# A conv, attention and expert kernel: the last half image's norm and gates moved into the experts, gate rows as single passes, constants made in layer 1

## The chip, the cores and the metric

The kernel runs on one core of a Trainium2 chip. Its time is the device time of one execution in microseconds. Three runs of the kernel before gave 3234.16, 3236.74 and 3243.24 us, median 3236.74. The profile shows one further execution, and every time of a single instruction here comes from that one.

## The reference, cut to what matters

Layer 0 is a convolution and attention block on 8 images of 256 channels and 32 x 32 points. Layer 1 works on 1024 tokens of 256 features per image: a causal attention, and then a mixture of 8 experts in which every token goes through every expert:

```python
t = t + attn(ln(t), WQ, WK, WV)
z = ln(t)
w = softmax(mean(z, axis=0) @ Wr + br)        # mean over the 8 images: one gate per token place and expert
h = relu(bn1(z @ W1[e] + b1[e]))
h = relu(bn2(h @ W2[e] + b2[e]))
t = t + sum_e w[:, e] * (h @ Wo[e] + bo[e])
```

The gate w needs the second norm z of all 8 images, because it is made from their mean. So the last image's second norm and the gate stand between the attention and the first gated product.

## The kernel before, in words

Tokens lie along the free axis, features on 128 partitions in KC = 2 groups; HALF = 512 tokens are half an image. Most operations go through a recording helper, so the profile shows them all at line 72, and they are told apart by their tiles.

**Layer 1** (from line 1276) takes the images in turn. `together` (446) runs two generators: `causal(b)` or `last()`, which is scores, softmax, transposes and product of image b, and beside it `beside(b)` (1558): the next image's first norm and keys, the previous image's second norm, and `chores`. A step's yielded number is its estimated cost, and the ratio 0.85 sets how much of the second generator goes between steps of the first. The order of the instructions on PE, DVE, ACT and POOL is the order of these calls. `layer_norm` (1342) transposes tokens onto partitions (`tpt`), takes mean and variance on DVE (`st`, `mv`), computes one over the root on POOL (`y`, `r`), scales (`zt`), and transposes back (`tpz`). `second_norm` (1418) adds the result to `feat` on POOL and gives it to `z_parts` (1432), which splits each number into an upper part (ACT), a lower part and a difference (DVE), so that a product of full precision is made of single-pass products; the three parts go to DRAM (`z_d`). `expert_parts` (1313) does the same for the experts' weights, by way of `we` and `parts_w`, as the 20 `chores`.

For the last image there is no next one to work beside. Its second norm is cut in two by `second_norm_half` (1442): half 0 and `gate(0)` (1532) are run beside the last attention products, and half 1 and `gate(1)` after everything else (1592 to 1594). `gate(h)` makes the scores `lg` (three products of 8 columns for each 128 tokens, in full fp32), a softmax over 8 experts on DVE and ACT, transposes it (`pwT`), and copies it into `wT`, 8 rows by 1024 tokens, in fp32.

**The experts** (from line 1609) first make `sel8` on POOL and `boT` by two transposes `pbo`. `sel8` holds, for each expert, an 8 x 128 matrix with ones in the expert's row: `gate_rows` (1663) multiplies it with `wT`, so that an expert's gates come to stand on all 128 partitions (`pw`, copied to `wb`). `gated_bias` (1670) multiplies `boT` with `wT` (`pg`, copied to `gb`). The folded norm constants `s1`, `s1a` and so on are written in this part of the program, but the scheduler had moved them to the start of layer 1.

Work is then 128 pieces: 2 groups of 4 experts, 2 halves, 8 images (32 visits of a half image), 4 experts in each. Piece n runs `layer1` of itself, `layer2` of piece n - 2 and `layer3` of piece n - 4, four steps each, interleaved; the DVE and ACT work that a step leaves goes into `soon`, for the same steps of the next piece. Each visit needs its z parts (`fetch_z`, tile `ze`, 1536 KB) and its t (`fetch_t`, tile `te`); visit 0's parts are loaded ahead into `z_first`. When a new half or group begins (b == 0), `gate_rows` is called at the start of its four pieces. PSUM has two banks of `pm` for layer 2, `pw` and `pg` together, and one each of the two `pa` (layer 1).

Tile pools stand in the way of early loads: the pools of the experts take the memory of layer 1's pools, so the first load into them waits until layer 1's last reader is done. The weights for (expert 0, all layers) and (expert 1, layer 1) and `z_first` lie in a pool of their own (`wm`) and are loaded before.

## Time and profile before

| | |
|---|---|
| median of three runs | 3236.74 us |
| the profiled execution | 3235.5 us |
| its span, first to last instruction | 3233.8 us |
| mean granted PE clock | 0.964 |
| PE busy | 2962.3 us (92%), 16822 instructions |
| DVE busy | 2385.1 us (74%), 3002 instructions |
| ACT busy | 1569.5 us (49%), 2312 instructions |
| POOL busy | 337.9 us (10%), 410 instructions |
| DMA | 237.46 MB, mean 73 GB/s |

Layer 1 runs from about 1428 to 2071 us, the experts from 2096.55 us to the end. Where a stretch of the profile is given as `A:B`, A and B are us from the span's start; after them come its length, then for PE, weight loads on PE, DVE, ACT and POOL the busy us with the number of instructions, then the mean granted clock, the share of the DMA engines and GB/s. A row of the timeline gives start, duration, engine, operation, output tile, inputs, shape and count, and in brackets the idle time ahead of it and what ended it.

### The profile page before, as it was taken

The page shows a single profiled execution, that of the slowest core. Times are in us where ns is not written, and L with a number is a line of the kernel's source. Part 1 is how long each engine was busy: PE and PEld are TensorE (multiplying, and loading weights), DVE is VectorE, ACT ScalarE, POOL GpSimd, SP SyncE. Part 2 cuts the span into 40 slices and gives each one's busy share as a digit, 9 for nine tenths or more (in the row PEclk, how much of TensorE's full clock was granted, in tenths as well). Part 3 has the DMA queues.
Part 4 walks back from the last instruction along what each step waited for, and adds up shares of the span by engine and source line. Part 5 has one row for each costly group of instructions (what it writes and reads, how often), then busy time and mean ns, then how long its engine had stood idle before and what let it go on. Part 6 is the DMA issues. An engine that isn't in the chain of part 4 may idle for free.

```text
span 3233.8 us, 41619 instructions
## 1 busy us (share of the span) xinstructions
PE 2962.3 (92%) x16822; PEld 1941.5 (60%) x16822; DVE 2385.1 (74%) x3002; ACT 1569.5 (49%) x2312; POOL 337.9 (10%) x410
## 2 busy tenths in 40 slices
PE   5998899989898999859999999799999999999998
PEld 3654545454555555435666555577767777777776
DVE  1378778777877878655666655488878888887887
ACT  1554455545445445313333333266656666666665
POOL 1121111121212110001122222100000000000000
PEclk9999999999999999989999999799999999999999
DMA  4203030303030300011323311322211242221220
GB/s 149 62 19 79 27 79 27 79 27 79 27 79 27 79 14 8 17 71 69 142 112 118 124 79 52 136 111 86 78 66 66 92 139 103 91 72 65 84 80 26
DMA packets 60061, 237.46 MB, mean 73 GB/s; under 512 B 5382, under 2 KB 13654, under 8 KB 50774
## 3 DMA queue, kind: packets, MB, share of 16 engines
q1 hardware_dynamic: 59862, 234.74, 21.5%
q8 instruction: 134, 2.20, 0.3%
q14 instruction: 65, 0.53, 0.0%
HBM read 143.23 MB, written 91.49 MB: 73 GB/s over the span
## 4 chain that ended last, share of the span: by engine, by line
PE 45%; DVE 7%; ACT 2%; issue 1%; POOL 1%; DMA 0%; SPq 0%; POOLq 0%; ACTq 0%; DVEq 0%
PE pm L72 12%; PE pa L72 11%; PE q L72 11%; PE s L72 4%; PE po L72 3%; PE pv L72 2%; DVE nm L72 1%; DVE pr L72 1%; PE pk L72 1%; DVE parts L72 1%; DVE zt L72 1%; ACT pr L72 1%; DVE st L72 1%; PE tpt L72 1%; PE pw L72 1%
## 5 line engine op out<-in xcount | busy, mean ns | idle before, releaser
L72 PE MATMUL q<-h2p,w 128*128 128x512 f32 x1536 | 485.9, 425 | 2.9 <-DVE h2p L72 1.7
L72 PE MATMUL pa<-ze,w 128*128 128x512 f32 x1488 | 422.5, 392 | 0.0
L72 PEld LDWEIGHTS q<-h2p,w 128*128 128x128 f32 x1536 | 288.9, 188 | 118.2 <-issue 60.4
L72 DVE SCALAR_TENSOR_TENSOR x<-hpad,vec,x 128x1024 f32<-128x1024 f32 x248 | 317.1, 1283 | 39.9 <-ACT x L72 32.8
L72 DVE SCALAR_TENSOR_TENSOR conv<-hpad,vec,conv 128x1024 f32<-128x1024 f32 x256 | 329.3, 1293 | 13.8 <-ACT conv L72 7.2
L72 PEld LDWEIGHTS pa<-ze,w 128*128 128x128 f32 x1488 | 278.9, 188 | 69.8 <-issue 9.5
L72 ACT ACTIVATE h<-pa,bn_o,s1a 128x512 f32<-128x512 f32 x256 | 198.8, 777 | 203.4 <-PE pa L72 203.3
L72 ACT ACTIVATE pT<-s 128x1024 f32<-128x1024 f32 x256 | 247.4, 1024 | 69.1 <-PE s L72 69.1
L72 DVE SCALAR_TENSOR_TENSOR h<-pa,s1b,h 128x512 f32<-128x512 f32 x256 | 191.6, 749 | 113.2 <-PE pa L72 100.8
L72 PE MATMUL po<-pT,vT 128*32 128x256 f32 x4096 | 272.1, 383 | 0.0
L72 PE MATMUL ph<-xn,piw 128*128 128x512 f32 x512 | 244.4, 615 | 3.1 <-DVE xn L72 1.6
L72 PE MATMUL s<-kk,z 128*128 128x512 f32 x512 | 245.2, 609 | 0.9 <-DVE pr L72 0.9
L72 PE MATMUL pm<-h,w 128*128 128x512 f32 x512 | 242.0, 595 | 0.0
L72 PE MATMUL pm<-h1p,w 128*128 128x512 f32 x768 | 216.1, 389 | 0.5 <-DVE h1p L72 0.5
L72 DVE SCALAR_TENSOR_TENSOR o<-vpad,pe_w,o 128x1024 f32<-128x1024 f32 x128 | 163.5, 1282 | 45.2 <-ACT o L72 42.0
L72 PE MATMUL s<-qst,kst 128*128 128x256 f32 x1024 | 175.2, 313 | 14.2 <-DMA kst<-part 12.9
L72 ACT ACTIVATE hpad<-ph,pi_o 128x512 f32<-128x512 f32 x126 | 86.9, 690 | 182.4 <-PE ph L72 182.4
L72 ACT ACTIVATE h2p<-h 128x1024 fp32r<-128x1024 f32 x128 | 134.9, 1054 | 77.8 <-DVE h L72 77.8
L72 PEld LDWEIGHTS po<-pT,vT 128*32 128x32 f32 x4096 | 120.2, 110 | 84.5 <-issue 1.9
L72 PEld LDWEIGHTS s<-qst,kst 128*128 128x128 f32 x1024 | 136.8, 192 | 47.5 <-issue 42.4
L72 PEld LDWEIGHTS pm<-h1p,w 128*128 128x128 f32 x768 | 144.1, 188 | 31.5 <-DVE h1p L72 0.9
L72 PE MATMUL pz<-pow__116,hid 128*128 128x256 f32 x512 | 138.2, 426 | 27.1 <-DVE hid L72 27.1
(241 smaller groups left out, 4811.7 us busy)
## 6 DMA issues: line engine op xcount, KB each, us to landing
ze<-zd SPq DMA_DIRECT2D x31, 1536.0 KB, 6.3
zd<-parts SPq DMA_DIRECT2D x16, 1536.0 KB, 5.5
qst<-part SPq DMA_DIRECT2D x32, 512.0 KB, 8.5
kst<-part SPq DMA_DIRECT2D x32, 512.0 KB, 15.2
te<-ud SPq DMA_DIRECT2D x32, 512.0 KB, 3.9
wd<-parts_w SPq DMA_DIRECT2D x20, 768.0 KB, 3.6
w<-wd SPq DMA_DIRECT2D x20, 768.0 KB, 5.9
t<-in_x_dram SPq DMA_DIRECT2D x8, 1024.0 KB, 4.9
```

What stands on the lines that cost most here:

```text
L72: return self._tc.keep_in_program_order(method(*args, **kwargs))
```

## The change

- **Half 1 of the last image**: `last_norm` does only half 0, in layer 1, into `z2_last`; its z parts are no longer made there. Half 1's t is stored, and loaded again into `scratch` in the experts' phase. There `last_half` runs the same `layer_norm` and `gate(1)` as a generator, two steps in every even piece from piece 4 on, at the second and fourth of its four steps. Seventeen steps bring it to piece 20. `feat` becomes two tiles.
- **z parts of the last image** are made when its visits come (visit 7 for half 0, visit 15 for half 1): `fetch_z` leaves its three steps in `soon`, and stores them for the second expert group.
- **Gate rows**: `wT` has 32 rows, four copies (upper, lower, upper, lower part of the gates), in a format that PE multiplies in a single pass. `sel8` selects an upper and a lower row, and `boT` has upper, upper, lower, lower parts. `stacked` makes these. `gate_rows` and `gated_bias` are called after the piece's four steps and not ahead of them.
- **Constants**: `sel8`, `boT` and the folded constants are made in layer 1, partly in the chores. `mhalf1` moves to the lasting pool.
- **Memory**: `we` has one buffer instead of two. `z_parts` has two parts in its tile and writes the difference over its source; the store becomes two stores. The second buffer for layer 2's parts is `z_first`.

Cut: `layer_norm` and `gate` move out of layer 1's block with their source, rows and banks as arguments; their steps are unchanged but for `stacked` in `gate`.

```diff
-    wT = wm.tile([NE, N], F32, name="wT")
+    wT = wm.tile([4 * NE, N], F32R, name="wT")
+    feats = [None, wm.tile([P, KC, HALF], F32, name="feat1")]
+    z2_last = wm.tile([P, KC, HALF], F32, name="z2_last")
...
+    def stacked(dst, src, order):
+
+        first = [order.index(i) for i in range(2)]
+        dve.tensor_copy(dst[:, :, first[0]].bitcast(F32R), src)
+        dve.tensor_sub(dst[:, :, first[1]].bitcast(F32R), src, dst[:, :, first[0]])
+        for i, part in enumerate(order):
+            if i not in first:
+                dve.tensor_copy(dst[:, :, i], dst[:, :, first[part]])
...
+        ge4 = room([P, nt, 4, NE], "ge4", 1)
+        stacked(ge4, ge, (0, 1, 0, 1))
+        yield 1.0
+        pwT = bank([4 * NE, HALF], "pwT")
+        for i in range(nt):
+            pe.transpose(pwT[:, i * P : (i + 1) * P], ge4[:, i].rearrange("p a e -> p (a e)"), ident)
...
+        boT = wm.tile([4 * NE, KC, P], F32R, name="boT")
+        sel8 = wm.tile([4 * NE, NE, P], F32R, name="sel8")
+        sel = two.tile([4 * NE, NE, P], F32, tag="pT", name="sel")
+        nc.gpsimd.memset(sel, 0.0)
+        for part in range(2):
+            nc.gpsimd.affine_select(
+                out=sel, in_=sel, compare_op=ALU.not_equal, fill=1.0, base=-NE * part,
+                pattern=[[-1, NE], [0, P]], channel_multiplier=1,
+            )
+        nc.gpsimd.tensor_copy(sel8, sel)
...
-                    w_ = two.tile([P, KC, C], F32, tag="we", name="we")
+                    w_ = two.tile([P, KC, C], F32, tag="we", name="we", bufs=1)
...
+            stacked(bo4, cols("bo").rearrange("p (e g) -> p g e", g=KC), (0, 0, 1, 1))
+            pb = bank([4 * NE, KC, P], "pbo")
+            for g in range(KC):
+                pe.transpose(pb[:, g, :], bo4[:, g].rearrange("p a e -> p (a e)"), ident)
+            dve.tensor_copy(boT, pb)
...
-            if b == 0:
-                pool.tensor_copy(feat, z2)
-            else:
-                pool.tensor_add(feat, feat, z2)
+            for h, feat in enumerate(feats):
+                half = z2[:, :, h * HALF : (h + 1) * HALF]
+                if b == 0:
+                    pool.tensor_copy(feat, half)
+                else:
+                    pool.tensor_add(feat, feat, half)
...
         def z_parts(b, h, src):
-            parts = two.tile([P, 3, KC, HALF], F32R, tag="parts", name="parts")
-            upper(parts, src)
+            parts = two.tile([P, 2, KC, HALF], F32, tag="parts", name="parts")
+            act.activation(parts[:, 0].bitcast(F32R), src, AF.Copy, scale=DOWN)
             yield 1.2
-            lower_part(parts, src)
+            dve.tensor_sub(parts[:, 1], src, parts[:, 0])
             yield 1.2
-            difference(parts)
+            dve.scalar_tensor_tensor(src, parts[:, 1], -STEP, parts[:, 0], ALU.mult, ALU.add)
             yield 2.4
-            nc.sync.dma_start(z_d[b][:, h], parts.bitcast(F32))
+            nc.sync.dma_start(z_d[b][:, h, :2], parts)
+            nc.sync.dma_start(z_d[b][:, h, 2], src)
...
+        def last_norm():
+
+            yield from until((B - 1, HALF // QC - 1))
+            yield from layer_norm(t[B - 1][:, :, :HALF], z2_last, rows_of_zt(), room, bank)
+            dve.tensor_add(feats[0], feats[0], z2_last)
+            nc.sync.dma_start(u_d[B - 1][:, :, :HALF], t[B - 1][:, :, :HALF])
+            yield 0.5
...
-                yield from second_norm_half(b, 0)
-                yield from gate(0)
+                yield from last_norm()
+                yield from gate(0, room, bank)
...
-        for steps in (chores, second_norm_half(B - 1, 1), gate(1)):
-            for _ in steps:
-                pass
+        for _ in chores:
+            pass
+        nc.sync.dma_start(u_d[B - 1][:, :, HALF:], t[B - 1][:, :, HALF:])
...
                 zs[v] = hp.tile([P, 3, KC, HALF], F32R, tag="z", name="ze")
-                nc.sync.dma_start(zs[v].bitcast(F32), z_d[b][:, h])
+                if (G, b) == (0, B - 1):
+                    parts, src = zs[v], z2_last if h == 0 else scratch[:, 2]
+                    soon[0].append(lambda: upper(parts, src))
+                    soon[1].append(lambda: lower_part(parts, src))
+                    soon[2].append(lambda: difference(parts))
+                    soon[3].append(lambda: later.append(lambda: nc.sync.dma_start(z_d[b][:, h], parts.bitcast(F32))))
+                else:
+                    nc.sync.dma_start(zs[v].bitcast(F32), z_d[b][:, h])
...
-            parts = h2_of[v, s] = hp.tile([P, 3, KC, HALF], F32R, tag="h2p", name="h2p")
+            parts = h2_of[v, s] = h2_parts[s % 2]
...
+        later = []
+        scratch = hp.tile([P, 3, KC, HALF], F32, name="scratch", bufs=1)
+        h2_parts = [hp.tile([P, 3, KC, HALF], F32R, name="h2p", bufs=1), zs[0]]
...
+        def last_half():
+
+            nc.sync.dma_start(scratch[:, 0], u_d[B - 1][:, :, HALF:])
+            yield
+            zt = scratch[:, 1].rearrange("p k (i c) -> p (k i) c", c=C)
+            yield from layer_norm(scratch[:, 0], scratch[:, 2], zt, room2, bank2)
+            dve.tensor_add(feats[1], feats[1], scratch[:, 2])
+            yield
+            yield from gate(1, room2, bank2)
+
+        extra = last_half()
...
-                if b == 0:
-                    gate_rows(G, h, s)
-                    if G == 0 and s < KC:
-                        gated_bias(h, s)
...
                     next(stage, None)
                 for step in now[i]:
                     step()
+                if n >= SLOTS and n % 2 == 0 and i % 2 == 1:
+                    next(extra, None)
+            for step in later:
+                step()
+            later.clear()
+            if n < len(pieces) and b == 0:
+                gate_rows(G, h, s)
+                if G == 0 and s < KC:
+                    gated_bias(h, s)
```

## The prediction

> **What bounds the kernel now.** I read first the slices of the page: TensorE (PE) is busy in nine tenths nearly everywhere, but for slice 26, where it falls to 7 with a granted clock of 7. That slice is the passage from layer 1's attention to the experts. So next the stretches around it, each ending at an event of the timeline (last attention product, first gate's transposes, second gate's transposes, first expert matmul `pa`, first gate row of piece 1, piece 4), and one full visit for measure. The columns are length, then busy us of PE, its weight loads, DVE, ACT and POOL, the clock, the DMA share and GB/s:

> ```profile
> 2060.13:2071.31 11.18, 7.59 (x38) 6.87 (x37) 5.21 (x9) 2.36 (x4) 0.00 (x0) 0.65 0.46 188
> 2071.31:2090.55 19.24, 10.77 (x45) 9.03 (x44) 8.68 (x21) 3.63 (x6) 2.07 (x6) 0.59 0.20 83
> 2090.55:2096.55 6.00, 4.14 (x8) 1.17 (x5) 1.01 (x2) 0.59 (x1) 2.04 (x2) 0.50 0.76 238
> 2096.55:2101.72 5.17, 5.16 (x13) 3.36 (x12) 0.75 (x1) 1.71 (x3) 0.00 (x0) 0.58 1.01 406
> 2101.72:2121.20 19.48, 19.07 (x65) 11.49 (x65) 10.74 (x12) 13.34 (x20) 0.00 (x0) 1.00 0.79 331
> 2121.20:2155.40 34.20, 34.20 (x137) 25.52 (x136) 28.05 (x31) 21.86 (x30) 0.00 (x0) 1.00 0.00 1
> ```

> In the visit (last line) PE has no idle time and DVE 6 us of it: the experts are bound by PE. In the first three lines, 36.4 us, nothing is bound: one chain hops from engine to engine. The chain of waits names it:

> ```profile
> 2063.05 5.70 PE lg L72 x24
> 2070.27 1.01 PE pwT L72 x4
> ...
> 2082.06 5.98 PE lg L72 x24
> 2089.54 1.02 PE pwT L72 x4
> 2090.69 0.92 POOL sel L1626
> 2091.65 1.14 POOLq L1929
> 2092.84 2.07 PE pw L72 x2
> 2094.91 1.71 PE pg L72 x2
> 2096.62 2.86 PE pa L72 x6
> ```

> So the second half's norm and gate stand alone from 2071.3 to 2090.5, then POOL writes `sel8`, then two gate rows run cold, and only then do the experts start. Last, from the timeline, a gate row in full flow and the worst one:

> ```profile
> 2386.92 1.12 PE L72 MATMUL pw<-wT,sel 8*128 8x512 f32 x2
> 2387.97 1.20 PE L72 MATMUL pa<-ze,w 128*128 128x512 f32 x4
> 2362.50 0.74 DVE L72 SCALAR_TENSOR_TENSOR h<-pm,s2b,h 128x512 f32<-128x512 f32 x1
> 2363.15 1.51 PE L72 MATMUL pg<-wT,boT 8*128 8x512 f32 x2 [0.68 <-ACT wb L72]
> ```

> and three visits as stretches (plain; first of h = 1; first of the second expert group):

> ```profile
> 2325.30:2359.50 34.20, 34.20 (x138) 25.49 (x137) 30.26 (x32) 21.16 (x29) 0.00 (x0) 1.00 0.23 77
> 2359.50:2404.80 45.30, 44.62 (x150) 28.63 (x149) 30.53 (x32) 24.78 (x35) 0.00 (x0) 0.92 0.16 58
> 2645.60:2684.10 38.50, 38.50 (x142) 25.70 (x141) 28.83 (x31) 22.81 (x32) 0.00 (x0) 1.00 0.57 198
> ```

> A row takes 1.05 us of PE (start to next start). The third of these visits holds four rows: 38.50 - 34.20 = 4.3. The second holds four rows and two `pg` of 0.95: 6.1 of its 11.1 us. The other 5.0: `pg` stands 0.68 us until DVE has emptied its bank (the row names ACT, but the 2362.50 line ends just then), and the clock is halved from about 2364 to 2371.

> **The change, part by part.** All against the profiled execution, 3235.5 us.

> *Out of the gap.* After the change's order PE goes from the first gate's `pwT` straight to `pa`, whose only wait is for a load that landed long ago. The 19.24 us go, and the 6.00 us go. Added to the chain are the four small DVE instructions that split the gates: neighbours of that size start 0.22 us apart, so 0.9 (0.6 to 1.2). `pa` starts at about 2072.2 instead of 2096.55: **-24.35**. z-parts of the first half (ACT 1.06, DVE 1.22 and 1.23) lay beside the gate's matmuls: nothing.

> *Gate rows in the opening.* Before, piece 0's rows ended in the gap; pieces 1, 2 and 3 paid 1.9 + 1.05 + 1.05 = 4.0. Now six single passes. The nearest row is a single-pass 128x512 `pa` (four in 0.91): 0.23 each, 1.4: **-2.6**. Rows of 32 instead of 8 partitions have no row here; between 0.2 and 0.45 each.

> *Loads.* They need the memory of layer 1, so they start where its last reader, `pwT`, ends: 2090.69 before, some 2072.2 now. But before they had a lead of 5.9 us on `pa`; now none. In the queue `w` of piece 2 stands between `te` (landed 6.6 us after the first issue) and a 256 KB weight (11.1 us); at the 430 GB/s of that stretch it landed about 10.5 us after it. PE asks for it after 5.17 (piece 0, cold) + 0.46 + 3.65 (piece 1, 2103.64 to 2107.29) + 0.46 = 9.7: a stand of **+0.8**. If the clock comes back sooner the stand grows by as much. Piece 4's `ze` lands at 22.2 (2097.27 + 15.6 - 2090.69), PE asks at 22.9: covered by 0.7 us only; later than that it would show at once. Sum so far -26.2.

> *The same norm and gate, spread over pieces 5 to 20.* PE is full there, so its part is paid: four groups of four transposes (0.45 warm, plus 0.2 for the change of format, which a row also shows: 1.05 against 2 x 0.43) 2.6; `lg`, 24 instructions in 5.7 to 6.0 at half clock, of which the first eight matmuls and loads, before the clock fell, ran at 0.65 per four: 4.0 (2.9 to 5.7); `pwT` 0.7. **+7.3** (5 to 10). DVE adds 7.7 us (statistics 2.4, scaling 1.4, sum 1.2, gate 2.7) over four visits with some 4 us free in each, ACT 3 us, at 62%: nothing; without that cover 7.7. Exp among the experts' Identity and Relu: between layer 1's Exp at 2069.23 and the experts' first Identity no table load appears, so nothing. In pieces 26 and 58 DVE makes z-parts (1.22 + 1.22) and ACT 1.05 in place of a load; DVE waits 2.1 us for `q` in the following piece today, so nothing, else 2 x 2.4. Their stores join SP's queue behind the piece, with nothing but the next `te` and result store behind them for pieces; `scratch` is loaded ahead of the `ze` of visit 2, wanted 34 us later. Odd pieces' h2 parts now go into `z_first`, last read in piece 3 and first rewritten in piece 4. Nothing for all three; 1.2 us of transfer (512 KB at 430 GB/s) if `scratch` delayed anyone.

> *Gate rows later.* Twelve `pw` at 1.05 against 0.25, two `pg` at 0.95 against 0.25: **-11.0**. They now stand behind a piece instead of ahead of it; the next `pa` is queued behind them on PE. At the end of piece 33 `pg` again finds a bank that DVE empties: by the same place in an earlier piece (`pm` ends 2138.2, DVE done 2139.3, PE there at 2138.8) a stand of 0.55.

> *The halved clock.* [...] By the row it began in the very window of the stand, and nowhere else in 1100 us of experts. I take the row: the fall goes, **-4.4**[...].

> *Layer 1.* POOL makes `sel8` at its start: memset 0.94, two selections of 1.10, a copy near 1.0, 4.1 in all, in its free time 1428.7 to 1441.8. DVE's four copies of `bo` lie in its idle time before 1437. The folded constants were already computed there. Two `pbo` transposes: 0.3. The difference of z-parts is now written into z2, so DVE waits for POOL's half sum (half of 4.52), which ends near 2029.9 where DVE comes at 2033.3: nothing, else 7 x 2 x 2.3. Two stores for one on SP (0.33 each to issue), behind which only the next store or load stands. One buffer for `we`: rival A. Together 0 (-2 to +4).

> Disturbance of full PE by nine inserted steps: +1.5 (0 to 37, see B).

> Sum: -24.35 - 2.6 + 0.8 + 7.3 - 11.0 - 4.4 + 1.5 = -32.8, giving 3202.7. The median of the runs lies 1.2 above the profiled execution: **3204**.

> **Rivals.** *A, slower: one `we` buffer.* Each of 20 weight parts of layer 1 may now load only when DVE has read the part before; the load takes 2.7 us at the median. If DVE waits it out each time, 54 us; once more than 61% of that reaches PE the change loses; all of it gives 3258. For it: DVE already waits seven times (21.7 us) for `parts_w` to be stored and once 5.4 for `we`. Against: the load is queued ahead of the same part's store, hence lands before that store (3.6), for which DVE waits anyway.
> *B: short stands cool the clock.* Each of nine inserted PE steps may stand 0.7 us and halve the clock for 6.8: 4.1 each. Four of nine: +16, 3220. For: the 45.30 visit. Against: every inserted step falls where even pieces use no bank of `pm`, and its input is two quarter pieces old.
> *C: the loads set the opening.* If they lose the whole lead of 5.9 us (landing later, or a halved clock after the stand of 0.8), 3210.
> *D: better.* `lg` at 2.9 (-1.1), format changes free (-1.0), no disturbance (-1.5), no stand for `w` or at piece 33 (-1.3), layer 1 at its better end (-2): 3197.

> **How the numbers follow.** Main case 0.56 (3198 to 3209), C 0.15, B 0.15, D 0.10, A 0.04. Down to 3194 and up to 3217 leaves out A, most of B and a part of D. 0.3%, 9.7 us, is about what a measurement can tell from none: slower needs A nearly whole, same a part of A or B at eight steps. Faster 0.95, same 0.02, slower 0.03.

> **What would show it.** In the new profile: `pa` starts about 12 us after the last `po` (before 36.4); rows of `pw` at 0.23 to 0.3; first visit of h = 1 near 36 us with clock 1.00; visits 1 to 4 longer by 7 to 9 us in all; `scratch` transposes without idle time ahead of them. Wrong if PE waits on `w` or `ze` for more than 2 us in the opening, if DVE's waits for `we` in layer 1 exceed some 20 us, or if the clock dips inside pieces 5 to 20.

## The result

The changed kernel takes **3209.86 us** (median of five runs, 3203.61 to 3212.5); the kernel before, run beside it, 3237.62. The difference of the medians is 27.8 us, and the ratio of the runs 0.9902 (95%: 0.9885 to 0.9918). The prediction was 3204.0, range 3194 to 3217: right in sign and range, 5.9 us too low.

The profiled execution of the changed kernel takes 3211.16 us, with a span of 3209.1. Its layers 0 and 1 ended 2.9 us later than in the profile before (last `po` 2063.06 against 2060.11), and layer 0's last store, up to which both kernels are the same, was already 3.6 later (1424.81 against 1421.19). In the profiles below, the end of the last `po` lies anywhere from 2052.3 to 2067.8. So what the change does is read from that end onwards: 3233.8 - 2060.11 = 1173.69 us before, 3209.1 - 2063.06 = **1146.04** after, 27.65 less, which agrees with the medians.

First the stretches of the changed kernel that answer to those shown of before: the gap from the last `po` to the first `pa`; piece 0 and its rows; piece 1 up to the `pa` of piece 2; from there to piece 4; the first visit of the second half; and the visit in which the second gate now lies. The columns are as before.

```profile
2063.06:2074.57 11.51, 7.35 (x38) 6.67 (x35) 3.44 (x11) 1.30 (x3) 0.00 (x0) 0.63 0.12 46
2074.57:2080.86 6.29, 6.15 (x17) 3.92 (x15) 1.74 (x3) 1.69 (x3) 0.00 (x0) 0.58 0.69 224
2080.86:2087.03 6.17, 3.96 (x16) 2.42 (x15) 2.52 (x4) 4.50 (x8) 0.00 (x0) 0.97 1.03 415
2087.03:2101.47 14.44, 14.39 (x46) 9.38 (x47) 8.82 (x10) 9.38 (x13) 0.00 (x0) 0.90 1.03 417
...
2349.10:2386.20 37.10, 36.86 (x142) 26.14 (x141) 30.39 (x33) 24.01 (x34) 0.00 (x0) 1.00 0.20 71
2206.00:2246.00 40.00, 39.93 (x162) 29.89 (x161) 32.70 (x44) 21.33 (x31) 0.00 (x0) 0.96 0.19 67
```

The gap has gone from 36.44 to 11.51 us. But from the first `pa` to the `pa` of piece 4 it is 26.90 us (the second to fourth lines), where before it was 2121.39 - 2096.55 = 24.84, by this row of before (the prediction ended the stretch at 2121.20, 0.19 too soon):

```profile
2121.39 1.07 PE L72 MATMUL pa<-ze,w 128*128 128x512 f32 x4
```

So the opening, as the text calls this stretch from here on, has become longer, though its six rows are cheaper. The third line says why: of 6.17 us PE is busy in 3.96, and the DMA share is 1.03, so loads take all the time of the DMA engines. The 45.30-us visit is down to 37.10 with the clock at 1.00, and a visit of 40.00 us with a clock of 0.96 is new. The chain of waits shows what ends last in the opening:

```profile
2065.93 5.81 PE lg L72 x24
...
2073.91 1.03 PE pwT L72 x4
...
2076.70 10.09 DMA w<-wd
...
2087.03 2.05 PE pa L72 x4
```

It is the gate, its transposes, and then a load of weights, not PE's own work. POOL and the rows are gone from between. A gate row in full flow, and the second bias row of the second half, from PE's timeline:

```profile
2368.62 0.50 PE L72 MATMUL pg<-wT,boT 32*128 32x512 f32 x1 [0.24 <-DVE h L72]
...
2378.21 0.49 PE L72 MATMUL pw<-wT,sel 32*128 32x512 f32 x1
2378.63 1.20 PE L72 MATMUL pa<-ze,w 128*128 128x512 f32 x4
```

A single pass takes 0.42 us from its start to the next, not 0.25.

By stretches, all in us, predicted against measured: the gap -24.35 against -24.93; the opening -2.6 + 0.8 = -1.8 against **+2.06**; from piece 4 to the end +7.3 - 11.0 - 4.4 + 1.5 = -6.6 against -4.78 (1112.41 to 1107.63). Together -32.8 against -27.65.

### The profile page after: what moved, and what is told of

Its sections match the earlier page's. It is cut to its first block, busy times and chain, and to the rows that moved or that the text cites. A ratio compares the mean times of both kernels' runs of the same rounds, so it can differ in the third digit from the quotient of the medians.

```text
span 3209.1 us, 41633 instructions
## 1 busy us (share of the span) xinstructions
PE 2950.3 (92%) x16802; PEld 1936.8 (60%) x16802; DVE 2380.9 (74%) x3014; ACT 1568.7 (49%) x2312; POOL 342.7 (11%) x419
## 3 DMA queue, kind: packets, MB, share of 16 engines
q1 hardware_dynamic: 63654, 232.12, 21.7%
## 5 line engine op out<-in xcount | busy, mean ns | idle before, releaser
L72 PE MATMUL pa<-ze,w 128*128 128x512 f32 x1488 | 422.8, 392 | 0.0
L72 DVE SCALAR_TENSOR_TENSOR x<-hpad,vec,x 128x1024 f32<-128x1024 f32 x248 | 317.1, 1283 | 40.6 <-ACT x L72 33.5
L72 DVE SCALAR_TENSOR_TENSOR conv<-hpad,vec,conv 128x1024 f32<-128x1024 f32 x256 | 329.3, 1293 | 15.5 <-ACT conv L72 8.9
L72 PEld LDWEIGHTS pa<-ze,w 128*128 128x128 f32 x1488 | 277.9, 188 | 63.2 <-issue 3.3
L72 ACT ACTIVATE h<-pa,bn_o,s1a 128x512 f32<-128x512 f32 x256 | 198.8, 777 | 207.3 <-PE pa L72 207.3
L72 ACT ACTIVATE pT<-s 128x1024 f32<-128x1024 f32 x256 | 247.5, 1025 | 72.0 <-PE s L72 72.0
L72 PE MATMUL po<-pT,vT 128*32 128x256 f32 x4096 | 273.4, 385 | 0.0
L72 PE MATMUL q<-h2p,w 128*128 128x512 f32 x768 | 269.4, 459 | 0.1
L72 DVE SCALAR_TENSOR_TENSOR h<-pa,s1b,h 128x512 f32<-128x512 f32 x256 | 191.4, 748 | 95.6 <-PE pa L72 87.0
L72 PE MATMUL s<-kk,z 128*128 128x512 f32 x512 | 247.9, 614 | 1.0 <-DVE pr L72 1.0
L72 PE MATMUL ph<-xn,piw 128*128 128x512 f32 x512 | 244.6, 615 | 3.1 <-DVE xn L72 1.6
L72 PE MATMUL pm<-h,w 128*128 128x512 f32 x512 | 240.9, 593 | 0.0
L72 PE MATMUL q<-z_first,w 128*128 128x512 f32 x768 | 216.5, 390 | 2.8 <-DVE z_first L72 1.7
L72 PE MATMUL pm<-h1p,w 128*128 128x512 f32 x768 | 217.0, 391 | 0.5 <-DVE h1p L72 0.5
L72 DVE SCALAR_TENSOR_TENSOR o<-vpad,pe_w,o 128x1024 f32<-128x1024 f32 x128 | 163.5, 1282 | 45.9 <-ACT o L72 42.7
L72 PEld LDWEIGHTS q<-h2p,w 128*128 128x128 f32 x768 | 144.5, 188 | 83.8 <-issue 59.6
L72 PE MATMUL s<-qst,kst 128*128 128x256 f32 x1024 | 176.1, 314 | 14.9 <-DMA kst<-part 13.5
L72 ACT ACTIVATE hpad<-ph,pi_o 128x512 f32<-128x512 f32 x126 | 86.9, 690 | 183.6 <-PE ph L72 183.6
L72 PEld LDWEIGHTS po<-pT,vT 128*32 128x32 f32 x4096 | 120.6, 110 | 85.6 <-issue 3.9
L72 PEld LDWEIGHTS s<-qst,kst 128*128 128x128 f32 x1024 | 137.6, 193 | 48.1 <-issue 42.7
L72 PEld LDWEIGHTS q<-z_first,w 128*128 128x128 f32 x768 | 144.2, 188 | 34.5 <-DVE z_first L72 2.9
L72 PEld LDWEIGHTS pm<-h1p,w 128*128 128x128 f32 x768 | 144.6, 188 | 32.1 <-DVE h1p L72 0.9
```

What stands on the lines that cost most here:

```text
L72: return self._tc.keep_in_program_order(method(*args, **kwargs))
```

## The experiments

Each kernel was run beside the kernel before (its median was 3237.37 for the first four, 3240.67 for the next four, 3239.45 for the last four). "From the last po" is the time from the end of layer 1's last product to the end of the program, in the profiled execution: 1173.69 before, 1146.04 changed. A visit is measured between the issues of two t loads; 34.2 is a plain one. A "stand" is time in which PE waits. Where tenths count, visits are taken from first `pa` to first `pa` instead: a plain one is 34.27 us so, in every one of the fourteen profiles.

**1. The first weights of expert 2 at the head of the queue** (changed kernel):

```diff
+        load_expert(hp, 2, 0)
         load_expert(hp, 1, 1)
         fetch_t(0)
```

> The changed kernel with one more line: the first weights of expert 2 (768 KB) are put at the head of the experts' load queue instead of standing third in it. Theory: the stand of 1.80 us for them ahead of piece 2 halves the clock for 3.4 us after it; both go, so from the first pa to the first pa of piece 4 26.9 becomes about 23.4 us, and the total falls by 3.5. Rival (the fall of the clock has another cause): only the stand goes, 25.1 us, total -1.8. Second rival (the loads behind the moved one are late in its place, such as the 768 KB of piece 1's second layer): 26.9 or more, total 0.

(The weights stood third among the weights, fourth in the queue.) Median 3202.15, ratio 0.9886 (0.9871 to 0.9901); from the last po 1142.92 (-3.1). The opening takes 24.26 us; the stand ahead of piece 2 (1.80 us in the changed kernel) is gone, and so is the halved clock after it (there 0.50 from 2086.62 to 2090.03). The theory's 23.4 was missed by two new stands, which PE's timeline names:

```profile
2085.43 1.17 PE L72 MATMUL pa<-z_first,w 128*128 128x512 f32 x4 [0.29 <-DMA w<-wd]
...
2092.89 1.20 PE L72 MATMUL pa<-ze,w 128*128 128x512 f32 x4 [1.20 <-DMA ze<-zd]
```

What the moved load gained was in part handed on to the loads behind it, `ze` above all. Run 8 follows from that.

**2. The second gate's narrow products in two halves** (changed kernel; one step more ahead of them, so that both halves lie in one even piece):

```diff
         nt = NT // 2
+        if h == 1:
+            yield 0.5
         lg = bank([P, nt, NE], "lg")
...
             pe.matmul(lg[:, i, :], ones[0:1, :], brs, start=False, stop=True)
+            if h == 1 and i == 1:
+                yield 1.0
```

> The changed kernel with the second gate's 12 products of 8 columns and 4 of 1 row issued as two halves of 1.7 us with a quarter of a piece of wide products between them, instead of 3.4 us in one go. Theory: 3.4 us of narrow products are too little work for the clock, and it halves for 3.4 us after them; in halves of 1.7 us it doesn't, so the fourth visit (40.0 us, clock 0.96) becomes about 38.2 with clock 1.00, and the total falls by 1.8. Rival (the fall comes from each stretch of narrow products, of whatever length): the clock falls twice, the visit takes about 41.8, total +1.8. Second rival (the fall has to do with something else at that time): 40.0 again, total 0.

Median 3206.38, ratio 0.9900 (0.9885 to 0.9915); from the last po 1146.19, no gain. The clock stayed at 1.00 in the visit, as the theory has it, and PE's busy time in the four visits fell by 1.05 us (144.38 to 143.33). But two stands of 0.25 and 0.42 us (for `h`, from ACT and DVE) are new behind the shifted steps, in run 3 too, and the four visits together went from 144.45 to 144.00 only. At the end of the program the clock fell once more in this execution, which took 1.1 us back. It fell behind a window that holds no narrow work, but stands for 49% of it (length, PE busy, instructions, clock, DMA share, GB/s):

```profile
3181.15:3184.57 3.42, 1.75 (x7) 1.00 0.00 0
3184.57:3187.98 3.41, 3.41 (x10) 0.50 0.00 0
```

The clock part of the theory holds, the gain doesn't.

**3. Both edits.**

> The changed kernel with both edits: expert 2's first weights at the head of the queue, and the second gate's narrow products in two halves. If both theories hold the gains add: -3.5 - 1.8 = -5.3, some 3204.5 by the median of the runs. If both fall by their rivals: -1.8 + 1.8 = 0, 3210.

Median 3202.26, ratio 0.9892 (0.9877 to 0.9907); from the last po 1142.63 (-3.4): the first edit's gain and 0.3. The median lies nearer to the first total than to the second, but it can't be told from that of run 1 alone; by the stretches it is run 1 plus run 2.

**4. The two bias rows of the second half together behind piece 32** (kernel before):

```diff
-                    if G == 0 and s < KC:
+                    if v == 0 and s < KC:
                         gated_bias(h, s)
...
                 for step in now[i]:
                     step()
+            if n == B * SLOTS:
+                for g in range(KC):
+                    gated_bias(h, g)
```

> The kernel before with one thing moved: the two bias rows pg of the second half stand together behind piece 32 instead of ahead of pieces 32 and 33, so that the second no longer meets a bank that VectorE still reads. All six rows keep their two passes and their cost. Theory (the stand of 0.68 us at pg halved the clock): the first visit of the second half falls from 45.30 us (clock 0.92) to about 40.3 (34.2 + 6.1 of rows, clock 1.00), total -5. Rival (a stand so short does nothing to the clock, the fall has another cause in that visit): about 44.6, the clock 0.92 again, total -0.7.

(The row that stood is the first of the two, ahead of piece 32; the text says the second. The edit takes the stand away all the same.) Median 3234.71, ratio 0.9989 (0.9982 to 0.9995); from the last po 1171.14 (-2.55 against before). The visit takes 42.73 us, clock 0.96. So neither text was right: without any stand the clock still halved, for 3.4 us instead of 6.8. PE's timeline shows it right behind the rows:

```profile
2375.24 1.98 PE L72 MATMUL pg<-wT,boT 8*128 8x512 f32 x4
2377.06 1.10 PE L72 MATMUL pw<-wT,sel 8*128 8x512 f32 x2
2378.09 1.81 PE L72 MATMUL pa<-ze,w 128*128 128x512 f32 x4
2379.70 1.91 PE L72 MATMUL pm<-h1p,w 128*128 128x512 f32 x4
```

PE has no idle time, and the two wide groups take 1.61 and 1.71 us to the next start where 0.91 is usual.

**5. The same two rows, each alone among wide products** (kernel before; the same first edit, and):

```diff
+                if (n, i) in ((B * SLOTS - 2, 3), (B * SLOTS, 1)):
+                    gated_bias(1, (n + 2) // (B * SLOTS + 2))
```

> The kernel before with the two bias rows pg of the second half put where each stands alone among wide products: one behind piece 30, one in the middle of piece 32. All six rows of the visit keep their two passes. With the pg together (the run before this one) no stand was left, and yet the clock halved for 3.4 us. New theory: matmuls that contract over 8 of 128 partitions are little work for the clock, and 2.7 us of them in one piece of time (with or without a stand among them) halve it for the next 3.4 us; one row of 1 us alone doesn't. Then the clock doesn't fall at all here: the visits on both sides of this place together 34.2 + 34.2 + 6 = 74.4 us, where the kernel before has 34.14 + 45.29 = 79.4, total -5. Rival (narrow rows lower the clock however far apart they stand, or the visit itself does): some 77 to 79, total 0 to -2.5.

Median 3236.83, ratio 0.9989 (0.9980 to 0.9998); from the last po 1170.31 (-3.4). The clock doesn't fall anywhere from piece 1 to the end. The two visits take 35.51 + 40.65 = 76.16 us, -3.3; that lies between the two sums of the text, and the clock decides: it is 1.00, as the new theory has it. What it had wrong is a row's price. Six rows cost 7.6 (76.17 - 2 x 34.27, from `pa` to `pa`), 1.27 each and not 1.05: a row also delays its own start by 0.09, and the `pa` behind it runs 0.12 longer.

**6. The norm back between layer 1 and the experts** (changed kernel; z of that half is stored at the end of layer 1 and loaded into `scratch`):

```diff
+        z2_half = two.tile([P, KC, N], F32, tag="z2", name="z2", bufs=1)[:, :, :HALF]
+        for _ in layer_norm(t[B - 1][:, :, HALF:], z2_half, rows_of_zt(), room, bank):
+            pass
+        dve.tensor_add(feats[1], feats[1], z2_half)
+        z2_d = dram.tile([P, KC, HALF], F32, name="z2_d")
+        nc.sync.dma_start(z2_d, z2_half)
+        for _ in gate(1, room, bank):
+            pass
...
-            yield from layer_norm(scratch[:, 0], scratch[:, 2], zt, room2, bank2)
-            dve.tensor_add(feats[1], feats[1], scratch[:, 2])
-            yield
-            yield from gate(1, room2, bank2)
+            nc.sync.dma_start(scratch[:, 2], z2_d)
```

> The changed kernel with one part undone: norm and gate of the last image's second half stand again by themselves between layer 1's last product and the experts; rows, constants and loads stay as changed. Theory: the gap grows by the 19.2 us that this chain took in the kernel before, and the four visits over which the work was spread lose their share of it: in the changed kernel they took 144.5 us from the second to the sixth t load, 4 x 34.2 = 136.8 without, so 7.7 less. Total +11.5. Rival (the 24 us gained in the gap came from sel8, boT and the rows, not from the norm): total 0 to +3.

Median 3218.59, ratio 0.9936 (0.9920 to 0.9953); from the last po 1153.90 (+7.9). The gap grew by 20.1 (31.65), the four visits lost 7.4 (137.04), as expected. What the theory had left out is the opening: 22.69 us instead of 26.90. The timeline shows the reason:

```profile
2082.41 0.33 SPq L1258 DMA_DIRECT2D w<-wd  x1
...
2089.15 2.55 PE L72 MATMUL pa<-z_first,w 128*128 128x512 f32 x6
```

The first load is issued 6.7 us ahead of the first `pa`; in the changed kernel it comes 0.5 us behind it (2075.05, 2074.57). The norm in the gap had covered the loads. Taking it out of the gap cost that cover. The norm's first transposes lie in pieces 4 and 6, ahead of the four visits; from piece 4 to the end it is 8.1 that went (1107.63 to 1099.58). So +20.1 - 8.1 - 4.2 = 7.8, the 7.9 measured but for rounding. (About 1 of the 4.2 is the clock, which here was back 2.0 us after the first `pa` instead of 5.2; what that is worth shows between runs 8 and 9, 22.66 and 23.64.)

**7. Rows of two passes at their new places** (changed kernel; `wT`, `boT` and `sel8` with 8 rows in full precision, no `stacked`, `pwT` of 8 rows):

```diff
-    wT = wm.tile([4 * NE, N], F32R, name="wT")
+    wT = wm.tile([NE, N], F32, name="wT")
...
-        ge4 = room([P, nt, 4, NE], "ge4", 1)
-        stacked(ge4, ge, (0, 1, 0, 1))
```

> The changed kernel with one part undone: gate rows and bias rows again in full precision, two passes over 8 partitions each, at their new places behind a piece; the gates are no longer split. Theory: a single pass takes 0.42 us of TensorE (0.33 where two stand together) against 1.05 (0.95), so 20 rows cost 16 x 0.63 + 4 x 0.62 = 12.6 more, the four small operations that split the gates leave the gap (-0.7), and where two rows of two passes stand together (the first visit of the second half) the clock may halve again (+1.7 to +3.4). Total +12 to +15. Rival (the single pass costs the 0.25 us at which the prediction priced it, 0.8 a row): +16. Rival (the rows hide behind weight loads, whatever their passes): 0 to +4.

Median 3219.14, ratio 0.9938 (0.9921 to 0.9954); from the last po 1157.17, +11.1. The gap lost 0.7, as expected (the clock fell 3.1 us behind the last `po` in both executions); the opening grew by 1.9 only, since the stand for weights shrank by 0.9 and piece 0 had its clock back 2.7 us sooner (4.65 us instead of 5.62); from piece 4 to the end +9.9, of which 1.5 are one more window of half clock behind the gate. That leaves 8.4 for 14 rows, 0.6 each: the theory's price. The rows are what the change says they are, at three quarters of the predicted saving. In the first visit of the second half the clock stays at 1.00, although its rows have two passes again: behind a piece they stand in pairs with wide work around, and no window there has more than 44% of them.

**8. Loads in the order in which they are wanted** (changed kernel):

```diff
-        load_expert(hp, 1, 1)
-        fetch_t(0)
-        for s in range(1, SLOTS):
-            for l in range(3):
-                if (s, l) not in w_in:
-                    load_expert(hp, s, l)
-        fetch_z(1)
+        load_expert(hp, 2, 0)
+        fetch_t(0)
+        load_expert(hp, 1, 1)
+        load_expert(hp, 3, 0)
+        fetch_z(1)
+        for s, l in ((2, 1), (1, 2), (3, 1), (2, 2), (3, 2)):
+            load_expert(hp, s, l)
```

> The changed kernel with the experts' loads in the order in which the pieces want them: first weights of expert 2, t, second weights of expert 1, first of expert 3, z of the second visit, then the others. With only the first of these moved to the front, the opening (first pa to first pa of piece 4) went from 26.9 to 24.26 us, with stands of 0.29 us for weights ahead of piece 3 and 1.20 for z ahead of piece 4. Theory (the opening is bound by when each load lands in the queue's order): both stands go, 22.8 us, total -4 against the changed kernel. Rival (the sum of the loads, 5.6 MB, binds, and the stand only moves to the second and third layers' weights in pieces 4 to 6): piece 4 is reached at 22.8 but the stretch to piece 8 is longer by as much, total -2.7.

(The 5.6 MB of the text are the eight weights alone; with t and z the ten loads have 7680 KB.) Median 3203.68, ratio 0.9894 (0.9877 to 0.9910); from the last po **1140.06**, the shortest of all (-6.0). The opening is 22.66 us, without a stand for any load. The rival fell: from piece 4 to the third t load it takes 42.23 us, in the changed kernel 42.28. The last 1.5 of the gain is chance: in this execution the clock didn't fall behind the gate, although its products are undivided.

**9. The gate's products computed twice** (kernel of run 8; the output stays the same):

```diff
-        for i in range(nt):
+        for i in [j for j in range(nt) for _ in range(1 + h)]:
```

> The kernel of the run before (loads in the order of their due times) in which the second gate's narrow products are each computed twice, 6.8 us in one go instead of 3.4; the output stays the same. New theory: [...] a window of which some 60% or more is narrow work or standing is followed by a half-clock window, one of which half or less is, is not. In the run before the 3.4 us fell half in one window and half in the next, and nothing happened. 6.8 us cover at least one window wholly and, unless they lie just so, more than 60% of a second: the clock falls for one or two windows, right behind the first covered one, so part of the products themselves and what follows run at half clock. The fourth visit grows by 3.4 for the products and by 1.7 to 3.4 for the clock: from 37.6 to 42.7 to 44.5. Rival (narrow products aren't what lowers the clock, something else at that place did it): 41.0, clock 1.00.

Median 3208.51, ratio 0.9907 (0.9891 to 0.9924); the visit 45.65 us, 1.2 over the upper end, because the clock stayed down for three windows. The 60% and the half of the text lie between shares measured up to run 8: windows of 56% and less were followed by a full one, of 62% and more by a half one, but for one window of 49% (table below). By a window is meant here a stretch of 3.413 us, as read from the changes of the granted clock: in the profile of the kernel before and in that of the changed kernel all of them lie whole multiples of 3.413 us apart, to 0.01 us. So in the changed kernel 2090.03 (up) and 2219.74 (down) are 129.71 us apart, 38 x 3.4134; before, 2100.93 (up) and 2363.75 (down) 262.82, 77 x 3.4133. Between the two profiles it is no multiple: 2100.93 lies 10.90 behind 2090.03, 0.66 more than 3 x 3.413. Cut along these times, PE's stretches of the changed kernel show (length, busy us, instructions, clock, DMA share, GB/s):

```profile
2216.33:2219.74 3.41, 3.41 (x23) 1.00 0.34 126
2219.74:2223.15 3.41, 3.41 (x9) 0.50 0.01 2
2223.15:2226.56 3.41, 3.41 (x16) 1.00 0.00 0
```

of run 8:

```profile
2206.23:2209.65 3.42, 3.35 (x20) 1.00 0.41 150
2209.65:2213.06 3.41, 3.41 (x20) 1.00 0.01 4
```

and of run 9:

```profile
2209.73:2213.14 3.41, 3.41 (x27) 1.00 0.32 123
2213.14:2216.55 3.41, 3.41 (x16) 0.50 0.00 0
2216.55:2219.97 3.42, 3.42 (x12) 0.50 0.00 0
2219.97:2223.38 3.41, 3.41 (x10) 0.50 0.01 2
```

But for 0.07 us in run 8, PE counts as busy throughout. In the changed kernel the narrow products (2215.83 to 2219.22) fill 85% of a window, and the next runs at half clock; in run 8 the same products (2207.95 to 2211.34) fall half and half on two windows, and nothing happens; in run 9 they fill one and more, and the clock falls right behind the first.

**10. Single-pass rows ahead of their piece** (changed kernel):

```diff
                 G, h, b = visits[v]
+                if b == 0:
+                    gate_rows(G, h, s)
+                    if G == 0 and s < KC:
+                        gated_bias(h, s)
...
-            if n < len(pieces) and b == 0:
-                gate_rows(G, h, s)
-                if G == 0 and s < KC:
-                    gated_bias(h, s)
```

> The changed kernel with one part undone: gate and bias rows, single passes as changed, stand ahead of a piece as in the kernel before. Theory: their place costs or gains little. The first piece's two rows fall back into the gap, where they also wait for VectorE's copy of the gates (+1.5 in the gap, given back in the opening by as much: rows gone from behind piece 0, and a stand for weights shorter by 0.8 or more). At piece 33 the second bias row meets a bank still being read for some 1.1 us; with two rows of 0.4 that is 1.9 of a window's 3.4, 55%, so the clock may or may not fall. Total 0 to +3. Rival (the place behind the piece is what removed the halved clock of the 45.30 us visit): the visit is back above 40, total +4 or more.

Median 3206.57, ratio 0.9906 (0.9890 to 0.9923); from the last po 1146.08, nothing. The gap is 2.3 longer, the opening 4.1 shorter (22.79 us; the stand for weights is down to 1.03), and behind the gate the clock fell for two windows instead of one, which with 1.1 us more in the visit (38.11) takes the rest. And the stand is back, ahead of piece 32:

```profile
2344.35 0.50 PE L72 MATMUL pw<-wT,sel 32*128 32x512 f32 x1
2344.89 0.58 ACT L72 COPY wb<-pw 128x512 f32<-128x512 f32 x1 [0.65 <-PE pw L72]
2345.50 0.74 DVE L72 SCALAR_TENSOR_TENSOR h<-pm,s2b,h 128x512 f32<-128x512 f32 x1
2345.52 0.50 PE L72 MATMUL pg<-wT,boT 32*128 32x512 f32 x1 [0.68 <-ACT wb L72]
2345.95 1.19 PE L72 MATMUL pa<-ze,w 128*128 128x512 f32 x4
```

It is the same 0.68 us as before the change, and the `pa` behind it takes the 1.03 that it takes behind any row: no fall. With run 4 this makes a pair: rows without the stand, and the clock falls; the stand with short rows, and it doesn't. The rows also show what the stand is. `pg` starts 0.05 us after ACT has copied `pw` out of its bank, when DVE's operation on `pm` has only begun: PE waits for ACT, as the row says, and not for DVE, as the prediction read it.

**11. `sel8` made by POOL at the start of the experts** (changed kernel; the same memset, two selections and copy, in `scratch`):

```diff
         scratch = hp.tile([P, 3, KC, HALF], F32, name="scratch", bufs=1)
+        sel = scratch[: 4 * NE, 1:].rearrange("p a k n -> p (a k n)")[:, : NE * P].rearrange("p (e n) -> p e n", n=P)
+        pool.memset(sel, 0.0)
...
+        pool.tensor_copy(sel8, sel)
```

> The changed kernel with sel8 made by POOL at the start of the experts again, but in memory of its own, not in layer 1. Theory: with the rows behind the piece, POOL has the 5.6 us of piece 0 to write it in (4.1 by the prediction), so nothing waits: opening 26.9, total 0. Rival (making it early is worth what the gap showed, 2 to 3 us of waiting for POOL): the first row stands 1 to 3 us, and the opening takes 28 to 30.

Median 3208.94, ratio 0.9913 (0.9896 to 0.9929). From the last po 1144.05 (-2.0, of which 1.7 is that the clock didn't fall behind the gate). The first row follows piece 0 after at most 0.2 us, the opening is 27.2: as the theory has it. Once the rows stand behind the piece, where the constant is made is worth nothing.

**12. One buffer for the weights split in layer 1** (kernel before):

```diff
-                    w_ = two.tile([P, KC, C], F32, tag="we", name="we")
+                    w_ = two.tile([P, KC, C], F32, tag="we", name="we", bufs=1)
```

> The kernel before with one thing changed: a single buffer for the experts' weights that layer 1 splits in parts, instead of two. The prediction's rival A said that VectorE might wait out 2.7 us for each of 20 loads, 54 us in all, and 58 us more in total if all of it reached TensorE. Theory: the load lands ahead of the store for which VectorE waits anyway, so its waits for these weights stay near 5 us, layer 1 is as long as before, total 0 (-2 to +2). Rival A: waits above 20 us and a total of +10 or more.

Median 3238.16, ratio 0.9999 (0.9989 to 1.0009): nothing. DVE's waits in layer 1 (us in total, times, longest) are these, in this kernel:

```profile
DVE parts_w L72 <- DMA we<-in_wo_dram: 17.5, 3, 6.5
DVE parts_w L72 <- DMA wd<-parts_w: 7.3, 4, 2.5
DVE parts_w L72 <- DMA we<-in_w_dram: 5.4, 1, 5.4
```

The waits for `we` did rise, to 22.9 us, over the theory's 5; but those for the store fell from 21.7 to 7.3, so DVE waits 30.2 us in place of 27.1. Layer 1 from its first transposes to the last `po` takes 624.5 us (before: 624.6). In the changed kernel itself the waits for `we` are 4.7 us. So rival A isn't there.

## Why the prediction was right, and where not

In the sum, the gap gained a little more than forecast, the opening and the later rows less. The total still lies inside the range, because the range had room for rival C; the main case's 32.8 us were 5 too many. Of the signs that it named, the start of `pa`, the 7 to 9 us more in the visits (8.4) and the transposes without idle time came as said. The rows (0.42 us, not 0.23 to 0.3) and the first visit of h = 1 (37.1, not 36) didn't, and the clock dipped in piece 17, which the prediction had named as a sign of being wrong.

**The gap** (-24.35): right, measured -24.93. The chain is the one that the order of instructions gives, and PE's wait for the gates ahead of `pwT` went from 1.52 to 2.18 us, so the four small operations cost 0.66, where 0.9 was estimated.

**The loads** (+0.8): the step that failed. The working saw that the lead of 5.9 us on `pa` was lost, and priced only the stand for the weights of piece 2. It had them land 10.5 us after the first `pa`, and PE ask for them after 9.7. They landed after 12.2, since the first load was issued 0.5 behind that `pa` and they took 11.7 from there; PE asked after 10.7. The stand measured 1.80, and the clock then halved for 3.4 us, another 1.5: with the due order and the clock coming back equally late (run 9: both 5.2 us after the first `pa`) the opening takes 23.64 instead of 26.90, 3.3 less. That is rival C, to which the prediction gave 3210 and a chance of 0.15, and what was measured is nearer to its time than to the main case's; its two parts, "landing later, or a halved clock after the stand", both came. In runs 2 and 11, where the clock came back 1.9 us sooner, the stand was 2.61 and 2.47 and the opening no shorter (27.13 and 27.20): the stand grew, as the prediction has it. Run 6 shows the exchange: the norm that the change took away was the loads' cover.

**Gate rows in the opening** (-2.6): also too good. A pair took 0.33 + 0.33, a single 0.42, 2.2 for six instead of 1.4, and piece 0 ran 5.62 us instead of 5.17, its clock being back later.

**Norm and gate on full PE** (+7.3, and +1.5 of disturbance): 8.8 together against 8.3, from `pa` to `pa` over visits 1 to 6 (the 144.45 us of the four visits leave out pieces 4 to 8, in which the first transposes lie). In the two executions in which the clock did not fall behind the undivided gate (runs 8 and 11) it is 6.7; `lg` took 3.4 us, not 4.0, and no transpose waited. The other 1.6 is the halved clock behind the gate, and whether that comes is chance, by the place of the gate in the windows. So the sum came out near, but not by its terms. Rival B had the clock fall at inserted steps, but by stands and at 4.1 each; it fell at one, by narrow work.

**Gate rows later** (-11.0): -8.4 by run 7. The prediction put a row of 32 partitions at 0.25, near the 0.23 of a wide product; it takes 0.42.

**The halved clock** (-4.4): the fall did go; the cause given for it was wrong, and the size too. The step put it down to the stand of 0.68 us. Runs 4, 5 and 10 refute that: the rows in two passes over 8 partitions were most of it (of the 3.41 us ahead of the fall at 2363.75 they took 1.7, the stand 0.68). Either half of the change was enough to take the fall away, the place alone in run 7, the single passes alone in run 10. So the forecast that it would go came true by luck. And the 5.0 us that it took the place to be worth is 3.3 by run 5, since rows cost 1.27 and not 1.05 (4.2 by run 7, where rows in pairs are cheaper).

What the runs show is a share of low work. The table gives, for windows at full clock, the share that is narrow work (products of 8 columns, or rows over 8 or 32 partitions) or a stand, and what the next window got. Up to 56% the next window was full, from 62% on it was half, in all fourteen profiles from the first `pa` to the last products, with one exception:

| share | where | next window |
|---|---|---|
| 45, 46, 47% | rows and stands (runs 2, 3, 10); half a gate (runs 2, 3) | full |
| 49 to 53% | the gate, half in each of two windows (runs 8, 11) | full |
| 56% | two two-pass rows in the opening (before, runs 4, 5, 12) | full |
| 62, 65, 69, 74% | the stand for weights in the opening, with rows or without (changed, runs 2, 11, 7) | half |
| 70, 71% | two-pass rows and the stand of 0.68 (before, run 12) | half |
| 74, 75, 81, 85, 100% | the gate (runs 10, 1, 7, changed, 9) | half |
| 84% | three two-pass rows without a stand (run 4) | half |

The 56% are the `pw` and `pg` of piece 1 in the kernel before; from its profile, in the columns of run 9:

```profile
2100.93:2104.34 3.41, 3.41 (x11) 1.00 1.04 431
2104.34:2107.75 3.41, 3.00 (x12) 1.00 1.01 423
```

The exception is the window of run 2 with 49% of stands and no narrow work, which was followed by half a clock, where 44% of stands (run 5) and 56% of narrow rows were not. That stands and narrow work of one share differ is shown by that one window alone. Which of few columns, few partitions or the many weight loads goes with the fall, the runs don't separate.

By stretches from piece 4 on, the parts now close: norm and gate +8.4 (with 0.1 of the last row), rows -8.4, the stand and the fall -4.2, and -0.6 in the last visit, whose cause is open: -4.8, as measured.

**Layer 1** (0): right. From its first transposes to the last `po` 623.5 us against 624.6; rival A fell (run 12).

**A version that beats both**: run 8, 3203.68 (0.9894). By the medians it can't be told from runs 1 and 3 (3202.15, 3202.26); by the time from the last `po` it is the shortest, 1140.06 against 1142.6 and 1142.9.

## What to carry to other kernels

Work that is taken off a critical gap may have been the cover of the loads behind it. Ask for each load in the queue when it lands and when it is wanted without that cover, and put the queue in the order of the due times: here that was worth 3.3 of the 27 us of the opening, with no work removed. A comparison of kernels that share a long part of equal code is best made from the end of that part: 3 us between two stretches were plain where the runs of one kernel lie 5 to 9 us apart. But a profile is one execution: what the clock did in it by chance, 1.6 us here, has to be taken out first.
